# Index lists later, masks as bits and padded node rows in a four-layer graph attention kernel

## The chip, the cores and the metric

The kernel runs on one core of a Trainium2 chip. The metric is the device time of one execution in microseconds. A core has five engines, each with an instruction stream of its own that it takes in order: TensorE (PE, matmuls), VectorE (DVE), ScalarE (ACT), GpSimd (POOL, which here does almost nothing but issue indirect gathers) and SyncE (SP, which issues most other DMAs). [...]

## The reference

Four layers of graph attention over 4096 nodes with 256 features, each followed by a residual sum and a layer norm. `adj` is a 4096 x 4096 matrix in which about one entry in 256 is set, and the diagonal.

```python
# layers 0 and 1: 4 heads of 64; layer 2: 2 heads of 128, with its own scores
h    = (x @ W.T).reshape(C, H, D).transpose(1, 0, 2)
e    = leaky_relu(alpha_src[:, :, None] + alpha_dst[:, None, :], 0.2)
e    = where(adj[None, :, :] == 0, -inf, e)
out  = einsum('hij,hjd->hid', softmax(e, axis=-1), h)
# layer 3: one head of 256, attention of +e and of -e, then one matrix
new  = concatenate([softmax(e) @ x, -softmax(-e) @ x], axis=1) @ fc_W
out  = elu(new)
# after each layer
x    = layernorm(x + out)
```

## The kernel before

A **row tile** is 128 nodes (32 tiles in all), a **block** is four row tiles. For a row tile only the nodes matter that have an edge into it, and since edges are rare, the kernel packs them: for each partition it lists which row of each node tile to fetch. `lists()` makes these index lists (`idx`, 13 columns for each row tile) on the chip out of `adj`: the raw matrix is fetched (L387), turned into bytes on ACT (`bytes`, L393), folded into bits on DVE (`squeeze`, L405), and ranks, places and sums on PE and DVE give the list, written at L522. It is a generator: each `next(lists)` puts one step in the program; five steps fetch and fold one block and then every row tile has four.

A **projection** (`Projection`, six steps from `transpose` to `store`) turns the features of a row tile into its node values: a row of 260, 258 or 514 numbers of weighted values plus a few score terms, stored in DRAM as `vals` (L702), from where gathers take it. Scores for the other side go into `edge` (L714). In layer 0 a row begins with 16 words of list bits (`BITS`), stored by `squeeze` (L410).

`RowTile.load` (L754 to L765) brings in what a row tile needs: its scores `S`, its mask, its own node values, and by 13 indirect DMAs on POOL (L763) the rows that its lists name, six for half 0 and seven for half 1. Gathers of half 0 may read only rows below `MIX * 128` (tiles 0 to 22); those of half 1 may read all. `RowTile.half` then makes the weights on ACT (L880, L847 in layer 3), masks them on DVE (L837, L882, L849, L851) and multiplies on PE (L898). In layers 0 and 1 the mask bytes lie in PSUM; in layer 0 they are unpacked from gathered bits (`unpack`, L798), copied out (L822) and stored as `maskC`, which layers 1 to 3 read back.

Some blocks are not packed but done **whole** (`WHOLE`: block 7 in layer 1; 3, 7 and 6 in layer 2; 7 and 6 in layer 3): all 32 node tiles are read in order as `vw`, with mask bytes `mw` from `maskW`, 512 KB for eight node tiles (L1158, L1230). These units are spread over the steps of the row tiles (`Layer.whole`).

`Program.run` sets the order. In the **head**, 32 projections of layer 0 run as a pipeline with one step of each of six tiles in a turn, and list steps are woven in. Then follow layer 0's row tiles, with two list steps around each half, then layers 1 to 3. `Layer.part` loads the row tile at hand and the next one or two; buffers are pools (`g0`, `g1`: four gathers' slots each), and a scheduler moves instructions within each engine's stream.

Of the kernel before, what the change touches and what calls it, by code (L numbers as in the profile page):

```python
# [50 lines left out]
P = 128  # L51
# [31 lines left out]
LEAD = 4  # L83
MIX = 23
CAP = NPAIR * P
BW = BT * P // 32
# [15 lines left out]
ROW = tuple(b + v + 2 * t for b, v, t in zip(BITS, VALS, TERMS))  # L102
KEXP = 10.0
# [19 lines left out]
def kernel(ctx: ExitStack, tc: tile.TileContext, ins: dict, out: bass.AP):  # L123
# [15 lines left out]
        "maskC": dram.tile([NT, P, NU, P], U8, name="maskC"),  # L139
        "maskW": dram.tile([NB, P, NT, BT, P], U8, name="maskW"),  # L140
        "d": [const.tile([P, NT, TERMS[n]], F32, name=f"d{n}") if WHOLE[n] else None for n in range(4)],
        "v": [[dram.tile([N + 1, ROW[n]], F32, name=f"vals{n}{c}") for c in range(1 if n else 2)] for n in range(4)],
# [36 lines left out]
class Program:  # L179
# [99 lines left out]
    def lists(self, ctx):  # L279
# [33 lines left out]
        nc.vector.memset(ones, 1.0)  # L313
        upto, past = (cst.tile([P, P], F16, name=name) for name in ("upto", "past"))
# [9 lines left out]
        for c in range(3):  # L324
# [9 lines left out]
        steps = column("steps", ((0, 3 * NT, P),), [(c * NT, 0) for c in range(3)]  # L334
                       + [(3 * NT + c, -(NT - 1) * P) for c in range(2)])
# [6 lines left out]
        pat = cst.tile([P, 8, P // 32], I32, name="pat")  # L342
# [16 lines left out]
        shared["pat"] = pat  # L359

        limit = cst.tile([P, NP], F32, name="limit")
        nc.vector.memset(limit[:, :2 * FIRST], float(MIX * P - 1))
        nc.vector.memset(limit[:, 2 * FIRST:], float(N))
# [9 lines left out]
        class Block:  # L373
# [21 lines left out]
            def squeeze(self, part):  # L395
                js = slice(part * JG, (part + 1) * JG)
                if any(self.blk in w for w in WHOLE):
                    nc.sync.dma_start(out=shared["maskW"][self.blk, :, js], in_=self.mk)
# [9 lines left out]
                if part == BT - 1:  # L408
                    rows = shared["v"][0][self.blk % 2][:N, :BW].rearrange("(j p) w -> p j w", p=P)
                    nc.sync.dma_start(out=rows, in_=self.bits.rearrange("p j t w -> p j (t w)").bitcast(F32))  # L410

# [49 lines left out]
        class Places:  # L461
# [45 lines left out]
            def sum(self):  # L507
                for pos in range(NP):
# [7 lines left out]
                    nc.tensor.matmul(PX[:, pos:pos + 1], self.under[:, c * P:(c + 1) * P], ones[:, :1], start=True,  # L516
# [83 lines left out]
    def run(self):  # L600
        ins, nc = self.ins, self.nc
        nothing = self.small.tile([1, max(ROW)], F32, name="nothing")
        nc.vector.memset(nothing, 0.0)
        for n in range(4):
            for v in self.shared["v"][n]:
                nc.sync.dma_start(out=v[N:N + 1, :], in_=nothing[:, :ROW[n]])
        w0 = self.weights(0)
        layer = Layer(self, 0)
        with ExitStack() as ctx:
            lists = self.lists(ctx)  # L610
            xs = []
            for q in range(NT // 2):
                if q % 4 == 0:
                    slot = self.g0.tile([P, SLOT], F32, name="G")
                c = 2 * F * (q % 4)
                nc.sync.dma_start(out=slot[:, c:c + 2 * F].rearrange("p (t f) -> p t f", t=2),
                                  in_=to_tiles(ins["x"][2 * q * P:2 * (q + 1) * P, :]))
                xs += [slot[:, c:c + F], slot[:, c + F:c + 2 * F]]

            line = [Projection(self, 0, w0, x, m, (self.ptwo[0], self.ptwo[1], self.pmask)) for m, x in enumerate(xs)]  # L620
            turns, ahead, listed = NT + 5, BT + 1 + 4 * LEAD, 0
            for m in range(turns):
                while listed < ahead and listed * turns <= m * ahead:
                    next(lists)
                    listed += 1
                for k, step in enumerate(Projection.STEPS):
                    if 0 <= m - k < NT:
                        step(line[m - k])

# [8 lines left out]
        self.mwp = self.pool("mwp", 2)  # L638
# [5 lines left out]
        layer.close(None)  # L644


class Projection:
# [36 lines left out]
    def row(self):  # L684
        nc, n, sh = self.nc, self.n, self.shared
        H, D, T, A, m = HEADS[n], WIDTH[n] - 1, TERMS[n], LOGS[n], self.m
        row = self.prog.io.tile([P, ROW[n] - BITS[n]], F32, name="row", bufs=3)
        vals = row[:, :VALS[n]].rearrange("p (h c) -> p h c", h=H)
        self.terms = row[:, VALS[n]:].rearrange("p (k t) -> p k t", k=2)
# [19 lines left out]
    def store(self):  # L709
        n, nc, T = self.n, self.nc, TERMS[self.n]  # L710
        erow = self.prog.io.tile([4, P], F32, name="erow")
        shift = self.shared["shift3"] if n < 3 else self.shared["zero"]
        nc.scalar.activation(erow[:T, :], self.pe[:T, :P], AF.Identity, bias=shift[:T, LOGS[n]:LOGS[n] + 1])
        nc.sync.dma_start(out=self.shared["e"][n][self.m], in_=erow[:T, :])  # L714
# [8 lines left out]
class RowTile:  # L723
# [23 lines left out]
    def load(self, half):  # L747
# [4 lines left out]
        if half == 0:  # L752
            self.S = prog.ld.tile([P, H4, P], F32, name="S")
            nc.sync.dma_start(out=self.S[:, :TERMS[n]], in_=sh["e"][n][m].partition_broadcast(P))  # L754
            self.mk = prog.ld.tile([P, NU, P], U8, name="mk")
            if n > 0:
                nc.sync.dma_start(out=self.mk, in_=sh["maskC"][m])
# [1049 lines left out]
```

## Time and profile before

| | us |
|---|---|
| median of 3 runs | 2065.5 (2065.28 to 2066.7) |
| profiled execution | 2071.33 |
| its span, first to last instruction | 2069.6 |
| PE / DVE / ACT / POOL busy | 1822.6 / 1467.9 / 1500.9 / 1383.9 |
| DMA moved | 486.59 MB, 235 GB/s |

The profile tells of one execution. Its engine times are busy times; waiting and issuing are not in them, so an engine can be the limit at 67%. Gathers are the 1352 instructions of L763; with 13 to a tile they tell which row tile POOL is at. In a line of the timeline the columns are start, duration, engine, line, operation, output and inputs, and how many; in brackets stands how long the engine had been idle and what ended that. In a table of stretches each engine has its busy time and its number of instructions, then come the granted PE clock, the DMA share and GB/s.

### The profile page before, as it was taken

The page shows a single profiled execution, that of the slowest core. Times are in us where ns is not written, and L with a number is a line of the kernel's source. Part 1 is how long each engine was busy: PE and PEld are TensorE (multiplying, and loading weights), DVE is VectorE, ACT ScalarE, POOL GpSimd, SP SyncE. Part 2 cuts the span into 40 slices and gives each one's busy share as a digit, 9 for nine tenths or more (in the row PEclk, how much of TensorE's full clock was granted, in tenths as well). Part 3 has the DMA queues.
Part 4 walks back from the last instruction along what each step waited for, and adds up shares of the span by engine and source line. Part 5 has one row for each costly group of instructions (what it writes and reads, how often), then busy time and mean ns, then how long its engine had stood idle before and what let it go on. Part 6 is the DMA issues. An engine that isn't in the chain of part 4 may idle for free. (4 is left out here: it accounts for less than half of the span.)

```text
span 2069.6 us, 46290 instructions
## 1 busy us (share of the span) xinstructions
PE 1822.6 (88%) x15281; PEld 1509.8 (73%) x15281; DVE 1467.9 (71%) x4366; ACT 1500.9 (73%) x4659; POOL 1383.9 (67%) x1387
## 2 busy tenths in 40 slices
PE   4765798999899959989989998899998999999995
PEld 2444677777778859978878788788986677667773
DVE  2434888888888959977777867778876366575655
ACT  4436888888877948866767769878874687667873
POOL 0016777777777777777777767777762776666772
PEclk7666998989989979998999999999999899999998
DMA  8677999999986867766666766777875898888983
GB/s 287 177 187 253 316 300 328 269 294 318 328 207 179 236 197 201 207 191 188 192 187 187 203 176 187 231 209 229 233 205 188 262 297 274 261 289 276 294 254 109
DMA packets 297816, 486.59 MB, mean 235 GB/s; under 512 B 77815, under 2 KB 206940, under 8 KB 297565
## 3 DMA queue, kind: packets, MB, share of 16 engines
q1 hardware_dynamic: 218076, 251.50, 40.1%
q0 software_dynamic: 74880, 227.83, 38.0%
q10 hardware_dynamic: 4608, 4.20, 0.6%
q8 instruction: 123, 2.02, 0.4%
q14 instruction: 129, 1.05, 0.2%
HBM read 427.36 MB, written 55.99 MB: 234 GB/s over the span
## 5 line engine op out<-in xcount | busy, mean ns | idle before, releaser
L763 POOL DMA_INDIRECT G<-vals,idx x1352 | 1378.4, 1020 | 653.4 <-issue 348.9
L898 PE MATMUL bank<-G,w 128*64 128x130 f32 (+5 forms) x9156 | 943.5, 311 | 73.6 <-DVE w L837 64.2
L898 PEld LDWEIGHTS bank<-G,w 128*64 128x64 f32 (+1 forms) x9156 | 769.8, 162 | 226.3 <-DVE w L837 73.3
L880 ACT ACTIVATE w<-S,G 128x64 f32<-128x64 f32 (+1 forms) x3080 | 823.5, 351 | 133.2 <-DMA G<-vals,idx 84.2
L1181 PE MATMUL bank<-vw,pw 128*128 128x129 f32 (+1 forms) x2560 | 419.8, 322 | 17.5 <-DVE pw L1171 5.8
L1181 PEld LDWEIGHTS bank<-vw,pw 128*128 128x128 f32 x2560 | 374.1, 194 | 58.2 <-issue 16.0
L837 DVE SCALAR_TENSOR_TENSOR w<-w,bank 128x1024 f32<-128x1024 f32 (+1 forms) x240 | 322.5, 1344 | 13.0 <-ACT w L880 12.4
L673 PE MATMUL bank<-wext,xT 128*128 128x268 f32 (+3 forms) x640 | 188.3, 429 | 33.5 <-DVE row L699 24.1
L673 PEld LDWEIGHTS bank<-wext,xT 128*128 128x128 f32 x640 | 123.2, 210 | 61.2 <-DVE row L699 24.7
L847 ACT ACTIVATE w<-S,G 128x64 f32<-128x64 f32 (+1 forms) x329 | 105.3, 352 | 85.5 <-DMA G<-vals,idx 51.0
L1171 DVE SCALAR_TENSOR_TENSOR pw<-pw,mw 128x512 f32<-128x512 f32 x192 | 129.9, 687 | 36.9 <-ACT pw L1170 35.5
L1178 DVE TENSOR_TENSOR pw<-pw,mw 128x512 f32<-128x512 f32 x128 | 87.6, 688 | 96.1 <-ACT pw L1175 62.8
L393 ACT ACTIVATE mk<-raw 128x1024 uint8<-128x1024 int32 x128 | 130.3, 1051 | 32.6 <-DMA raw<-in_adjB_dram 32.3
L876 DVE TENSOR_TENSOR w<-S,G 128x384 f32<-128x384 f32 x180 | 92.4, 517 | 79.8 <-DMA G<-vals,idx 61.0
L1170 ACT ACTIVATE pw<-Sw,d 128x512 f32<-128x512 f32 x192 | 134.5, 710 | 15.5 <-PE bank L1181 10.2
L1244 PE MATMUL bank<-vw,pw 128*128 128x65 f32 x512 | 89.1, 257 | 19.9 <-issue 19.9
L1173 ACT ACTIVATE pw<-Sw,d 128x512 f32<-128x512 f32 x128 | 89.9, 708 | 19.3 <-DMA Sw<-edge 10.3
L1246 PE MATMUL bank<-pw,vw 128*65 128x128 f32 x512 | 99.5, 277 | 0.0
L1244 PEld LDWEIGHTS bank<-vw,pw 128*128 128x128 f32 x512 | 78.6, 194 | 27.6 <-issue 27.3
L1241 DVE SCALAR_TENSOR_TENSOR pw<-Sw,cw,mw 128x512 f32<-128x512 f32 x128 | 93.8, 740 | 0.0
L664 ACT COPY xT<-bank 128x256 f32<-128x256 f32 x128 | 46.3, 362 | 62.3 <-PE bank L659 41.0
L706 PE MATMUL bank<-ident,row 128*4 128x128 f32 (+2 forms) x128 | 37.6, 294 | 56.6 <-DVE row L693 30.5
(193 smaller groups left out, 1805.1 us busy)
## 6 DMA issues: line engine op xcount, KB each, us to landing
raw<-in_adjB_dram SPq DMA_DIRECT2D x128, 512.0 KB
G<-vals,idx POOLq DMA_INDIRECT x1352
mw<-maskW SPq DMA_DIRECT2D x36, 512.0 KB
vw<-vals SPq DMA_DIRECT2D x128, 128.5 KB
S<-edge SPq DMA_DIRECT2D x60, 256.0 KB
vals<-row SPq DMA_DIRECT2D x96, 134.0 KB
vw<-vals SPq DMA_DIRECT2D x96, 129.0 KB
xp<-y SPq DMA_DIRECT2D x96, 128.0 KB
```

The lines of the kernel that those rows point to most:

```text
L393: nc.scalar.activation(self.mk[:, 2 * q:2 * q + 2], src, AF.Copy)
L673: nc.tensor.matmul(pp[:, :c1 - c0], self.xT[:, k, :], wext[:, k, c0:c1], start=(k == 0), stop=(k == KT - 1 and brow is None))
L763: nc.gpsimd.indirect_dma_start(out=self.row(half, k), out_offset=None, in_=self.values[:N + 1 if half else MIX * P, :], in_offset=bass.Ind ...
L837: nc.vector.scalar_tensor_tensor(pair, pair, LEAST, mh2, op0=ALU.max, op1=ALU.mult)
L847: nc.scalar.activation(w[0][:, u, rows], S[:, 0, rows], AF.Relu, bias=d(g, 0))
L880: nc.scalar.activation(w[h][:, u, rows], S[:, h, rows], AF.Exp, bias=d(g, h))
L898: nc.tensor.matmul(a, w[h][:, u, rows], b, start=half == 0 and u == 0 and (n == 3 or h == turns[0][0]), stop=half == 1, skip_group_check=True)
L1170: nc.scalar.activation(p, S[:, h], AF.Exp, bias=d)
L1171: nc.vector.scalar_tensor_tensor(p, p, LEAST, mj, op0=ALU.max, op1=ALU.mult)
L1181: nc.tensor.matmul(accs[it][:, c:c + Wd], p[:, it, :], v[:, c:c + Wd], start=(j == 0 and h == heads[0]), stop=(j == NT - 1), skip_group_ch ...
L1244: nc.tensor.matmul(bu[:, it * Wd:(it + 1) * Wd], p[up][:, it, :], v[:, up * Wd:(up + 1) * Wd], start=j == 0 and it == 0, **how)
L1246: nc.tensor.matmul(bf[:Wd, it * P:(it + 1) * P], v[:, flat * Wd:(flat + 1) * Wd], p[flat][:, it, :], start=j == 0 and it == 0, **how)
```

## The change

1. *Head.* `LEAD` goes from 4 to 3: 17 list steps stand ahead of layer 0 for 21. Nine of them are woven into the first 24 turns of the projections (all 21 were spread over 37 turns), and eight follow after the projections. `x` comes in six DMAs for sixteen, layer 0's `edge` rows are stored four tiles at a time, the five small stores of zeros move from SP to ACT, and layer 0 prefetches one row tile ahead for two. `LATE` keeps a bound that `LEAD` had set.
2. *Masks.* `maskC` and `maskW`, bytes in DRAM, become `bitsC` and `bitsW`, 32 times 128 bits. Layer 0 copies out the gathered bits (28 words a half) and no longer the bytes; layers 1 to 3 unpack them on DVE for every half, and whole blocks for every node tile.
3. *Rows.* Node values stand `PITCH` apart: 320 words (1280 bytes) in layers 0 to 2, 520 words in layer 3, before 284, 268, 262 and 516. Indices are multiplied by 5 and count fifths of a row. Gathers move as many bytes as before; stores of `vals` write the pad, which is set to zero.

```diff
-LEAD = 4
+LEAD = 3
+LATE = 4
+MW = P // 32
+STRIDE = 5
+PITCH = tuple(-(-r // (u * STRIDE)) * u * STRIDE for r, u in zip(ROW, (64, 64, 64, 1)))
...
-            turns, ahead, listed = NT + 5, BT + 1 + 4 * LEAD, 0
+            turns, soon, listed = NT + 5, BT + 5, 0
             for m in range(turns):
-                while listed < ahead and listed * turns <= m * ahead:
+                while listed < soon and listed * 24 <= m * soon:
                     next(lists)
                     listed += 1
                 for k, step in enumerate(Projection.STEPS):
                     if 0 <= m - k < NT:
                         step(line[m - k])
+            for _ in range(BT + 1 + 4 * LEAD - listed):
+                next(lists)
...
-            for q in range(m, m + (3 if self.n == 0 else 2)):
+            for q in (m, m + 1):
...
+        nc.vector.memset(row[:, ROW[n] - BITS[n]:], 0.0)
...
-            self.mk = prog.ld.tile([P, NU, P], U8, name="mk")
+            self.bits = prog.ld.tile([P, 2 * HALF, MW], I32, name="bits")
             if n > 0:
-                nc.sync.dma_start(out=self.mk, in_=sh["maskC"][m])
+                nc.sync.dma_start(out=self.bits, in_=sh["bitsC"][m])
...
-                out=self.row(half, k), out_offset=None, in_=self.values[:N + 1 if half else MIX * P, :],
+                out=self.row(half, k), out_offset=None, in_=self.values[:N + 1 if half else MIX * P, :].rearrange("r (k c) -> (r k) c", k=STRIDE),
...
+        bits = self.bits[:, half * HALF:(half + 1) * HALF]
+        if L.n == 0:
+            t = self.m % BT * MW
+            rows = self.slot(half, 0)[:, :HALF * ROW[0]].bitcast(I32).rearrange("p (k c) -> p k c", k=HALF)
+            L.nc.vector.tensor_scalar(bits, rows[:, :, t:t + MW], 0, None, op0=ALU.bitwise_or)
+            if half == 1:
+                L.nc.sync.dma_start(out=L.shared["bitsC"][self.m], in_=self.bits)
...
-            if n == 0:
-                self.unpack(half, there.rearrange("p (t i) -> p t i", t=U))
-                nc.vector.tensor_scalar(kept, there, 0, None, op0=ALU.bitwise_or)
-                if half == 1:
-                    nc.sync.dma_start(out=sh["maskC"][self.m], in_=self.mk)
-            else:
-                nc.vector.tensor_scalar(there, kept, 0, None, op0=ALU.bitwise_or)
+            self.unpack(half, there.rearrange("p (t i) -> p t i", t=U))
+        else:
+            there = prog.mkp.tile([P, UNITS[1], P // 4], I32, name="mk")[:, :U]
+            self.unpack(half, there)
...
+    def block_bits(self, blk):
+        bits = self.prog.mwp.tile([P, NT, BT, MW], I32, name="bw")
+        self.nc.sync.dma_start(out=bits, in_=self.shared["bitsW"][blk])
+        return bits
+
+    def bytes(self, bits, j):
+        mj = self.prog.mup.tile([P, BT, P // 4], I32, name="mw")
+        spread(self.nc, mj, bits[:, j], self.shared["pat"])
+        return mj.rearrange("p t i -> p (t i)").bitcast(U8).rearrange("p (t i) -> p t i", t=BT)
```

`spread` is one DVE product: each word of bits, repeated over eight bit planes, is combined by `bitwise_and` with a pattern, which gives mask bytes. `unpack` calls it three times for a half, `bytes` once for a node tile.

## The prediction

> **What bounds the kernel now.** I read the table of stretches first, cut at the first GpSimd gathers of each layer (13 per row tile, so 416, 364, 260 and 312 for layers 0 to 3).
>
> ```profile
> core 0: us, PE busy (x) PEld busy (x) DVE busy (x) ACT busy (x) POOL busy (x), PEclk, DMA share, GB/s
> 125.00:165.00 40.00, 30.41 (x201) 19.71 (x201) 18.11 (x62) 12.17 (x39) 5.96 (x6) 0.59 0.66 144
> 165.00:698.00 533.00, 466.91 (x4671) 386.42 (x4670) 430.01 (x1279) 449.26 (x1524) 406.36 (x410) 0.88 0.94 281
> 698.00:1178.00 480.00, 428.11 (x4452) 383.28 (x4451) 381.91 (x982) 341.20 (x1300) 369.10 (x364) 0.94 0.70 196
> 1178.00:1545.00 367.00, 342.91 (x2988) 315.01 (x2989) 276.44 (x790) 290.76 (x865) 278.48 (x260) 0.97 0.75 214
> 1545.00:2070.00 525.00, 483.66 (x2640) 358.78 (x2636) 317.70 (x1091) 348.56 (x800) 319.53 (x313) 0.96 0.78 248
> ```
>
> No engine is full by this table, though POOL is: its timeline and the tile view of `vals` show why.
>
> ```profile
> L763 POOL DMA_INDIRECT G<-vals,idx x1352: 940/946/2292, 125.2 to 2036.3; - x194
>   issue: 348.9, 1112
> ...
> 131.74 0.95 POOL L763 DMA_INDIRECT G<-vals,idx  x1 [0.30 <-issue]
> 165.34 0.94 POOL L763 DMA_INDIRECT G<-vals,idx  x1 [32.65 <-DMA edge<-erow]
> 166.59 0.94 POOL L763 DMA_INDIRECT G<-vals,idx  x1 [0.30 <-issue]
> ...
> 1543.56 0.94 POOL L763 DMA_INDIRECT G<-vals,idx  x1 [0.30 <-issue]
> 1589.17 0.94 POOL L763 DMA_INDIRECT G<-vals,idx  x1 [44.67 <-ACT row L691]
> ```
>
> A gather takes 0.946 us and is followed by 0.304 us in which POOL waits for nothing: 1.25 us, 16.25 us for a tile's 13. From 165.3 to 1544.5 this runs on almost without another gap. So until layer 2 ends, the time is the start of this stream plus the number of gathers; whatever starts it earlier or lengthens a gather counts in full. The other waits in it are only the 9 us of one layer change. Layer 3 is different: PE is 92% busy, the chain of waits alternates between L898 and L1181, both PE, and POOL waits for PE to free slots.
>
> The stream starts at 165.3, not at 125.2, because half 1 of tile 0 may gather from all rows and so needs the last row stored:
>
> ```profile
> 147.49 1.53 SPq L702 DMA_DIRECT2D vals<-row  x2
> 161.31 0.79 SPq L702 DMA_DIRECT2D vals<-row  x2
> 162.76 0.80 SPq L702 DMA_DIRECT2D vals<-row  x2
> ```
>
> Layer 0 hides a second limit. The first three unpack products of a half (L798) mark where compute stands: 144 of them, 24 tiles, lie between 222.7 and 646.9, 17.67 us a tile, while POOL took 16.96 (24 tiles between 207.1 and 614.2). Compute falls behind, and what lets POOL run on is that its index lists are written early:
>
> ```profile
> 591.43 0.17 DVE L522 TENSOR_TENSOR idx<-bank,limit 128x13 int32<-128x13 f32 x1
> 597.72 0.94 POOL L763 DMA_INDIRECT G<-vals,idx  x1 [0.30 <-DVE total L454]
> ```
>
> That is tile 26: 6.3 us of lead. DMA isn't what slows compute there: the waits between 300 and 590 us are between PE, DVE and ACT, and the largest on a DMA is 4 us, though the DMA share is 1.0.
>
> **What the Trainium skill says.** "Perfetto Trace Analysis", section "DMA Instruction — SWDGE (GPSIMD)": the end of such a record is the end of descriptor generation, not of the transfer. The trace agrees: the median is 946 ns whether a row has 1048 or 2064 bytes. So the wider pitch should leave POOL's 1.25 us alone. "SBUF — State Buffer", section "SBUF: two separate sides": a VectorE operation with two SBUF inputs and a GpSimd operation exclude each other on a shared port. The trace agrees in size: gathers beyond 0.946 us sum to 369.1 - 364 x 0.946 = 24.8 us in layer 1 and 278.5 - 260 x 0.946 = 32.5 us in layer 2, where such products (L1241 and about half of L876, 137 us; L1171 and L882, 190 us) run: 0.17 to 0.18 us lost per us of product. "DMA: Bandwidth & Descriptors", section "How a descriptor splits into AXI transactions": a read that doesn't start on 256 bytes fetches an extra piece. Rows 1136, 1072 and 1048 bytes apart mostly start off it; 1280 always starts on it, 2080 doesn't. No view here isolates that.
>
> **The change part by part.** *Head.* In the built order, ACT makes its 24th mask conversion (L393, at 80.9 us before) with 9 of 32 rows begun; after, 14. The last 18 rows then have six single conversions between them, where the last 23 had 13 to 16 and the list work of tiles 1 to 5. Also gone before the last row: the second 64-byte store of list bits (issued 127.6; ACT then stood 8.45 us for a row store). Undisturbed rows took 1.6 us each (seven from 105.4 to 115.0). Sum: 80.9, less 2 (five small stores leave SP's queue, x comes in 6 DMAs for 16), plus 5 rows x 1 us of transfers, plus 18 x 1.6 = 29, plus 6 x 2 for a conversion and its wait, plus 3 for landing: 128. The stream starts 37 us earlier.
>
> *Layer 0.* The lists are postponed, not removed. Built order: an index list stood 2.0 to 2.5 unpacked tiles ahead of use; after, 1.0 to 1.67. Taking one tile, 17.7 us, off the lead shown (22 to 28 us around tile 8, 6 at tile 26), POOL must wait from about tile 10, and the layer goes at compute's pace. So the gain is compute's. Its first exponentials (L880) were at 177.0; after, six conversions and the bits store stand before them, so about 16 us past the new start: 144, gain 33. Tiles 0 to 3 now carry lists (before, six lists were ready): -6. Each tile then saves 0.2 us of DVE: the copies L822 go (0.283 + 0.312), two copies of 28 words come (priced as the 0.156 us of L693) and a pad memset (0.06): +5 over 24 tiles. Lists end one tile later and the last list holds POOL: -5. Layer 1 starts 27 us earlier. If the lead holds after all, 37; if the head gains less, 10.
>
> *Masks as bits, layers 1 to 3.* Per row tile six products: 2 x 0.213 + 3 x 0.192 + 0.260 = 1.26 us (L798 by form); per whole-block step one of 128 words, 0.28 (L416). Layer 1: 28 x 1.26 + 64 x 0.28 = 53 us of DVE, of which the removed L826 gives back 17. Layer 2: 20 x 1.26 + 96 x 0.28 = 52. Layer 3: 24 x 1.26 + 128 x 0.28 = 66. DVE has room (80, 75 and 61% busy), so the time itself lies beside gathers and matmuls; the cost is gathers lengthened. Short products may slip between a gather's accesses (0) or cost as the long ones do (0.18, or 0.35 as an upper end, twice that). I take 0.15: 8 us in layer 1, 8 in layer 2. The layer change at 1545 to 1589, where PE is full and DVE at 85%, takes 3; layer 3, PE-bound, 2. Together 21 us, 12% of the 171 added.
>
> *Transfers.* Counted from the issue list: mask bytes written and read were 6.3 + 18.9 + 4.7 + 10.6 = 40 MB; the bits take about 5.4; pads add 2.4. Some 33 of 487 MB go. Nothing that ends POOL's stream waits for them: cost and gain zero, bounds 0 and -10 (shorter landings in layer 3, where ACT waited 51 us for gathers). Grouped edge stores, pad memsets in layers 1 to 3 and the prefetch of two tiles for three: zero, behind POOL.
>
> *Sum.* -27 + 21 = -6 on the execution's own 2071.3 us (span 2069.6). The median of the runs is 2065.5, so 2059.5; I say 2059.
>
> **The rivals.** *A, slower: DVE's added work gets on the path.* Its place is layers 1 to 3. Layer 0 shows that compute falls behind POOL with DVE 81%, ACT 84% and PE 88% busy; layer 2 would have DVE at 89% and PE at 93%. If a quarter of the 171 us lands on the path, 43 - 27 = +16: 2081. It decides from 16% (27/171). Against it: after its opening stall layer 2 did some tiles in under 14 us. *B: layer 0 swallows the head.* If compute starts late and lists cost more, the gain is 10: 10 - 21 = +11, 2076. For it: layer 0's pace; against: fewer conversions really precede the last row. *C: transfers matter more.* Aligned reads and 33 MB less shorten landings, POOL's lead holds: -37 - 10 + 13 = -34, 2031. Against: no DMA wait in the views is on POOL's stream. That the pitch cuts rows into several descriptors, lengthening each gather, I give almost nothing: only the index's coefficient changes in the instruction.
>
> **How the numbers follow.** Forecast 0.47 (2045 to 2072 by the terms' own bounds), A 0.25, B 0.12, C 0.16. The range 2036 to 2084 leaves out a tenth on each side. No change can be told within 0.2%, 4 us. Forecast: 0.29 faster, 0.10 same, 0.08 slower; A 0.02, 0.02, 0.21; B 0.02, 0.02, 0.08; C 0.15, 0.01, 0. Sum 0.48, 0.15, 0.37.
>
> **What would show it.** The seventh gather near 128 us; waits of POOL on DVE from tile 10 of layer 0; layer 1's first gather near 671; mean gathers of 1.04 us in layer 1 and 1.10 in layer 2; layer 3's length unchanged within 5 us. Wrong would be: a seventh gather after 145, no POOL waits in layer 0, or a layer 2 whose compute trails POOL by more than a tile.

## The result, and the profile after

The changed kernel takes 2166.1 us (2159.5 to 2168.8, four executions) where the kernel before took 2065.4 (2064.1 to 2066.7): a ratio of 1.048, 95% interval 1.046 to 1.051. The forecast was 2059. On two of the chips used below the kernel before itself took 2733 and 2779 us, so the experiments from there are compared only with others on the same chip.

The chain of row starts reads best from the first gather of each layer. All numbers are us from the start of the profiled execution; layer 3's length runs to the end of the span.

| | 7th gather | layer 1 starts | layer 1 | layer 2 | layer 3 | span |
|---|---|---|---|---|---|---|
| before | 165.3 | 698.2 | 480.0 | 411.0 | 480.4 | 2069.6 |
| after | 126.4 | 767.1 | 480.4 | 407.7 | 508.0 | 2163.1 |

The head gives 39 us. Layer 0 then takes 640.7 us from its seventh gather to layer 1's first, where it took 532.8: 108 us lost. Layers 1 and 2 are as long as they were, within 4 us, and layer 3 is 28 us longer. The two losses are in two places. For both the runs point to the order of instructions within the engines; for the first this is shown by a single edit, for the second it is inferred.

This is the table of stretches of the changed kernel, cut at the seventh gather, at the first gathers of layers 1 and 2, and where layer 2's gathers end.

```profile
core 0: us, PE busy (x) PEld busy (x) DVE busy (x) ACT busy (x) POOL busy (x), PEclk, DMA share, GB/s
126.00:767.00 641.00, 496.73 (x4876) 405.72 (x4877) 441.40 (x1365) 458.87 (x1552) 399.30 (x410) 0.83 0.75 226
767.00:1247.00 480.00, 430.09 (x4456) 378.88 (x4456) 405.25 (x1198) 338.31 (x1295) 369.29 (x364) 0.95 0.65 183
1247.00:1613.00 366.00, 340.41 (x2958) 311.63 (x2954) 300.72 (x1021) 290.02 (x855) 286.64 (x261) 0.97 0.67 190
1613.00:2163.00 550.00, 494.48 (x2616) 355.94 (x2616) 363.57 (x1363) 347.32 (x797) 330.69 (x313) 0.95 0.73 218
```

In layer 0 no engine is near full: PE is busy 497 us of 641 and VectorE 441. The layer is longer because all of them wait. The list of waits between 200 and 760 us (engine and line, what it waited for, us in all, times, longest) says on what:

```profile
engine line waited for: us in total, times, longest us
PEld bank L911 <- DVE w L850: 125.2, 54, 11.5
...
DVE bits L809 <- DMA G<-vals,idx: 102.3, 22, 10.3
...
POOL G L785 <- DVE idx L528: 72.5, 5, 14.8
```

TensorE waits for VectorE's mask product, VectorE waits at the copy of the bits (L809) for gathers, and GpSimd waits for VectorE to write an index list (L528). That is a ring. The page's group line of the copy shows how cheap it looks if only its own time is read (busy us, mean ns, then idle time of the engine before it):

```profile
L809 DVE TENSOR_SCALAR bits<-G 128x28 int32<-128x28 int32 x64 | 11.3, 178 | 129.4 <-DMA G<-vals,idx 122.5
```

64 copies cost 11.3 us of work and 122.5 us of standing. One turn of the ring, in the timelines of GpSimd and VectorE around the gathers of tile 13 and tile 14 (start, duration, and in brackets the idle time before with its releaser):

```profile
388.24 0.95 POOL L785 DMA_INDIRECT G<-vals,idx  x1 [0.31 <-issue]
403.96 0.94 POOL L785 DMA_INDIRECT G<-vals,idx  x1 [14.77 <-DVE idx L528]
...
385.89 0.29 DVE L409 SCALAR_TENSOR_TENSOR bits<-fold 128x128 int32<-128x128 int32 x1
394.11 0.18 DVE L809 TENSOR_SCALAR bits<-G 128x28 int32<-128x28 int32 x1 [7.92 <-DMA G<-vals,idx]
...
403.51 0.17 DVE L528 TENSOR_TENSOR idx<-bank,limit 128x13 int32<-128x13 f32 x1 [2.28 <-ACT counts L443]
```

Tile 13's last gather ends on GpSimd at 389.2. VectorE waits for its data until 394.1 and only then makes the copy. The work queued behind the copy takes until 403.5, when the list of tile 14 is written; tile 14's first gather follows at 404.0. No gather of tile 14 could overlap those of tile 13. Over four tiles (first gathers of tile 12 and tile 16: 348.99 and 437.08) this makes 88.1 us where 4 x 16.25 = 65 would do, so 23 us are lost in these four tiles.

The **built order**, the fixed sequence in which each engine takes its instructions, shows that this is no accident of timing; the trace has the same sequence. In VectorE's stream the list of tile 14 is the 20th instruction behind the copy of tile 13's second half, and the lists of tiles 10, 18, 22 and 26 stand just so. List 10 stands behind the copies of tiles 0 to 9, and lists 13 and 14, 17 and 18, and so on up to 26 stand behind all copies of the tile before.

In the kernel before, the products that unpack the gathered bits (L798) write the one bank of masks, and the copy L822 read that bank, so neither came early. Sums that need only gathered rows and scores (L876) stood in VectorE's stream too, but between 200 and 690 us VectorE waited for gathers 4.3 us in all, where it now waits 102.3 at the copy alone. When a list is written there, the mask products done are 2.5 to 3.0 tiles behind it.

### The profile page after: what moved, and what is told of

It reads as the page before. It is cut to its first block, busy times and chain, and to the rows that moved or that the text cites. A ratio compares the mean times of both kernels' runs of the same rounds, so it can differ in the third digit from the quotient of the medians.

```text
span 2163.1 us, 46803 instructions
## 1 busy us (share of the span) xinstructions
PE 1843.4 (85%) x15281; PEld 1505.3 (70%) x15281; DVE 1559.7 (72%) x5159; ACT 1497.8 (69%) x4659; POOL 1396.3 (65%) x1387
## 4 chain that ended last, share of the span: by engine, by line
PE 46%; POOL 12%; DVE 11%; DMA 11%; ACT 10%; issue 8%; SPq 1%; DVEq 0%; POOLq 0%; ACTq 0%
PE bank L911 24%; POOL G L785 12%; PE bank L1192 11%; DMA G<-vals,idx 8%; ACT w L893 6%; PE bank L690 4%; DVE w L850 3%; ACT mk L399 1%; ACT pw L1181 1%; PE bank L1255 1%; DMA raw<-in_adjB_dram 1%; PE bank L1253 1%; PE bank L522 1%; PE bank L524 1%; DVE pw L1182 1%
## 5 line engine op out<-in xcount | busy, mean ns | idle before, releaser
L911 PE MATMUL bank<-G,w 128*64 128x130 f32 (+5 forms) x9156 | 964.7, 314 | 177.6 <-DVE w L850 141.9
L1192 PE MATMUL bank<-vw,pw 128*128 128x129 f32 (+1 forms) x2560 | 413.7, 320 | 11.5 <-DVE pw L1182 4.0
L809 DVE TENSOR_SCALAR bits<-G 128x28 int32<-128x28 int32 x64 | 11.3, 178 | 129.4 <-DMA G<-vals,idx 122.5
L1250 DVE SCALAR_TENSOR_TENSOR pw<-Sw,cw,mw 128x512 f32<-128x512 f32 x128 | 93.1, 743 | 0.0
```

Source lines behind the costliest of these rows:

```text
L911: nc.tensor.matmul(a, w[h][:, u, rows], b, start=half == 0 and u == 0 and (n == 3 or h == turns[0][0]), stop=half == 1, skip_group_check=True)
L1192: nc.tensor.matmul(accs[it][:, c:c + Wd], p[:, it, :], v[:, c:c + Wd], start=(j == 0 and h == heads[0]), stop=(j == NT - 1), skip_group_ch ...
```

## The experiments

Each experiment is an edit of the changed kernel unless it says otherwise. The stage lengths of all are in one table at the end of this section.

### The list lead, or the copy

The first pair changes the lead of the lists, with the prefetch of three tiles that goes with it, and then the place of the copy in the program's text, with the products reading the gathered rows directly.

```diff
-LEAD = 3
+LEAD = 4
...
-            for q in (m, m + 1):
+            for q in range(m, m + (3 if self.n == 0 else 2)):
```

> The changed kernel with the list lead put back: 4 x 4 list steps ahead instead of 4 x 3 before layer 0 starts, and layer 0's prefetch of three tiles instead of two; the head's early weave and everything else stay. Theory 1 (a postponed list is late at POOL): POOL's five waits on the index write, 72 us, go; layer 1's first gather comes near 690 instead of 767, and the total near 2089. Theory 2 (the copy of the gathered bits, which stands in VectorE's order ahead of the next list and waits for a transfer, makes the loop): the lead moves only the first waits, layer 1 starts near 750 and the total stays above 2145. Layer 3 keeps its 508 us under both.

Measured: 2191.4 us, ratio to before 1.061 (1.057 to 1.064), layer 1 at 800.8. A longer lead is no cure; GpSimd waits 90.7 us for lists in nine places instead of 72.5 in five. In the built order lists are now 2.5 to 3 tiles ahead of the mask products, as before the change, but lists 13, 14, 17, 18 and so on still stand behind the copies of the tile just before. The layer became 34 us longer than with lead 3. In the trace lists 12, 16, 20 and 24 now stand behind a copy of the tile just before too, and GpSimd stands idle for 8 us before each of these tiles, which it did not with lead 3.

```diff
-            L.nc.vector.tensor_scalar(bits, rows[:, :, t:t + MW], 0, None, op0=ALU.bitwise_or)
-            if half == 1:
-                L.nc.sync.dma_start(out=L.shared["bitsC"][self.m], in_=self.bits)
+            kept, bits = bits, rows[:, :, t:t + MW]
...
         spread(L.nc, words[:, u:u + len(FULL[half]), :], bits[:, k:k + len(FULL[half])], pat)
+        if L.n == 0:
+            L.nc.vector.tensor_scalar(kept, bits, 0, None, op0=ALU.bitwise_or)
+            if half == 1:
+                L.nc.sync.dma_start(out=L.shared["bitsC"][self.m], in_=self.bits)
```

> The changed kernel, list lead 3 as it is, but layer 0's products read the masks in the gathered rows directly, as before the change, and the copy of the bits for layers 1 to 3 follows the products instead of preceding them. Theory 2: VectorE's wait of 109 us at the copy goes, layer 1 starts near 700, total near 2100. Theory 1: the products wait for the same transfer at the same place; layer 1 starts within 10 us of 767 and the total within 0.5% of 2166. Layer 3 keeps its 508 us under both.

Measured: 2165.3 us, 1.047 (1.043 to 1.051), layer 1 at 775.7. Taken at its word this would speak against the copy. But the built order shows that the edit moved nothing: the scheduler places instructions by what they need, the copy needs only the gather, and it stands ahead of the same lists as in the changed kernel (10, 13, 14, 17 and so on). The experiment did not test what it was made for. To move the copy, its place has to be held by an **edge**: a dependency that lets one instruction be issued only after another.

### Which part of the change brings the loss

The next two take one part back: the head (lists, loads of x, edge stores, lead and prefetch as before), and the pitch.

```diff
-            for tiles in (2, 2, 4, 8, 8, 8):
+            for q in range(NT // 2):
...
-            turns, soon, listed = NT + 5, BT + 5, 0
+            turns, soon, listed = NT + 5, BT + 1 + 4 * LEAD, 0
...
-        k = self.m % 4 if n == 0 else 0
+        k = 0
```

> The kernel before with masks as bits and the wide pitch, without the head (list steps, lead, prefetch, loading of x and edge stores as before). If the loss of layer 0 comes from the head's lead alone: first seven gathers at 165, layer 1 near 698, layer 2 near 1178, layer 3's 508 us stay, total near 2093. If the copy of the bits makes it: layer 1 at 730 or later, total above 2120. If layer 3's 27.6 us come from the head, layer 3 takes 481 and the total is near 2066.

Measured: 2200.0 us, 1.064 (1.060 to 1.068), layer 1 at 812.9, layer 3 at 501.7. Without any of the head, and with its lead of 4, layer 0 loses more than with it. So the head isn't the cause in either place.

```diff
-STRIDE = 5
-PITCH = tuple(-(-r // (u * STRIDE)) * u * STRIDE for r, u in zip(ROW, (64, 64, 64, 1)))
+STRIDE = 1
+PITCH = ROW
```

> The changed kernel with node values at the old distance (1136, 1072, 1048 and 2064 bytes), head and bits kept. The forecast's reading, that the pitch moves nothing on the path: within 0.3% of 2166, layer 3 at 508. If the pitch shortens landings that layer 0's loop waits for (3.87 to 3.18 us was seen): layer 1 starts later by up to 32 x 0.7 = 22 us, 2188. If the pitch of 2080 bytes makes layer 3 longer: layer 3 at 481, 2139.

Measured: 2235.7 us, 1.082 (1.078 to 1.086). Layer 1 starts at 862.0, 95 us later, a result that no expectation covered; layer 3 takes 476.5 us. Layer 3's loss comes with the pitch, then, and in layer 0 the bits cost even more without it. The trace shows where: the lists stand behind the same copies, but ten more of VectorE's instructions stand between copy and list (30 for 20 at tiles 10, 14, 18, 22 and 26, and 13 for 3 at tiles 13, 17, 21 and 25), so that the four tiles from 12 on take 98.4 us for 88.1. GpSimd's idle times before tiles 4 to 6 (23.5, 11.8 and 17.3 us for 4.0, 1.4 and 5.1) are most of the rest.

### Holding the copy in its place

The same edit as in the second experiment, with one edge: the copy may not be issued before the last product of its half.

```diff
-        spread(L.nc, words[:, u:u + len(FULL[half]), :], bits[:, k:k + len(FULL[half])], pat)
+        last = spread(L.nc, words[:, u:u + len(FULL[half]), :], bits[:, k:k + len(FULL[half])], pat)
+        if L.n == 0:
+            with L.prog.tc.issue_after(last.ins):
+                L.nc.vector.tensor_scalar(kept, bits, 0, None, op0=ALU.bitwise_or)
```

It was made at lead 3, at lead 4 with the prefetch of three tiles, and at lead 4 without the pitch.

> The changed kernel with one edge of order more: layer 0's products read the masks in the gathered rows, and the copy of the bits is held behind the last of these products of its half on VectorE. The list lead stays at 3. In the built order the copies then stand 1.0 to 2.0 tiles behind the list they used to stand in front of by 0 to 1.0. Theory of order (a copy that waits for tile k-1's gathers stands ahead of the write of list k, so that gathers of two tiles in four can't overlap): the waits of POOL on the index write fall below 25 us in all and layer 1's first gather comes near 700 instead of 767, total near 2100. Rival, the list lead of 3: VectorE would wait at the first product instead, layer 1 after 745, total above 2144. Layer 3 stays at 500 to 510 us under both.

> The same edge, with the list lead of 4 and layer 0's prefetch of three tiles put back; the head's early weave stays. Theory of order: layer 0 keeps its old pace and the 39 us of the head arrive, layer 1's first gather near 665 (698 less 39, plus lists that come later), total near 2065. Rival, that the bits cost VectorE time on the path: layer 1 not before 700. Against the run with lead 4 and the copies in front (800 us, 2191) the edge alone would be worth 130 us.

> The run with the copies held behind and lead 4, with the old distances of 1136, 1072, 1048 and 2064 bytes. If the pitch works in the memory (layer 0 at 862 without it against 767 with it): layer 1's first gather 30 us or more later than in the run with the pitch. If that too was a matter of order: layer 1's first gather within 10 us of that run. Layer 3 at 476 to 482 us, so the total near 2035 in the second case.

On the chip on which the kernel before took 2733 us, these three measured 2774.6, 2770.4 and 2728.3, ratios of 1.015 (1.009 to 1.022), 1.015 (1.011 to 1.020) and 0.998 (0.996 to 1.001). Layer 1 started near 1000 us in all, so they decided nothing on layer 0. They were run again.

> The same kernel as in the run with the copies held behind and lead 4, again, because in that call the kernel before itself took 2733 us instead of 2066, with long waits that no semaphore shows. Theory of order: layer 1's first gather near 665, layer 3 at 500 to 510 us, total near 2065. Rival, that the bits cost VectorE time on layer 0's path: layer 1 not before 700.

Measured: 2041.9 us, 0.986 (0.983 to 0.989), layer 1 at 647.5, 50.7 us earlier than in the kernel before and 153 earlier than with lead 4 and the copies in front. The view of the copy's line in this run:

```profile
L820 DVE TENSOR_SCALAR bits<-G x64: 165/175/181, 152.2 to 655.3; 128x28 int32<-128x28 int32 x64
its engine sat idle before it (us, times) until:
who waited for it (us, times):
```

The copies still take 0.175 us each, and the list of waits before them is empty. The table of stretches has the rest: layer 0 from the seventh gather on now takes 523 us, with the busy times of the changed kernel within 7% on every engine.

```profile
core 0: us, PE busy (x) PEld busy (x) DVE busy (x) ACT busy (x) POOL busy (x), PEclk, DMA share, GB/s
124.00:647.00 523.00, 464.77 (x4868) 380.45 (x4868) 444.11 (x1369) 458.52 (x1550) 398.38 (x410) 0.91 0.89 277
```

> The kernel with the copies held behind at a list lead of 3, again, because in its first call every kernel was slowed. If lead 3 with copies behind suffices: layer 1 within 10 us of the 647.5 of lead 4, total near 2045. If the lead costs something of its own, as the forecast had it (POOL waits for lists from tile 10 on, layer at compute's pace, 12 us of the head lost): layer 1 at 660 to 675, total near 2060. If the lead were the main cause: layer 1 after 700.

Measured: 2047.2 us, 0.993 (0.991 to 0.995), layer 1 at 654.7. This run and the second experiment differ by the edge alone: it is worth 118 us of the total and 121 of layer 1's start (on their two chips the kernel before took 2062 and 2069 us). The lead of 3 costs 6 us of layer 0 against the lead of 4, not the main part. With lead 3 a list is written as little as 0.3 us before its first gather (tiles 6, 18 and 22), with lead 4 at least 7.1 from tile 6 on; GpSimd stands 1.2 us at most for it, at tile 6 with lead 3.

> The same kernel as before without the pitch, copies held behind, lead 4, again for the same reason. If the pitch works in the memory: layer 1's first gather 30 us or more later than in the run with the pitch. If the 95 us that the pitch was worth in layer 0 were the loop's: within 10 us of it. Layer 3 at 476 to 482 us; total near 2035 in the second case.

Measured: 2034.5 us, 0.984 (0.981 to 0.987), layer 1 at 659.2, layer 3 at 478.2. So most of the pitch's 95 us was the ring's; 12 us remain, 7 of them before the seventh gather (131.3 against 124.0).

> The kernel without the head (first lists, loads of x, edge stores and lead as before the change), masks as bits with the copies held behind, wide pitch in fifths of a row. If the head's gain is the 39 us of the seventh gather: layer 1 near 647 + 39 = 686, and the total near 2081 with layer 3's 508. If the head is worth less than its seventh gather shows: layer 1 nearer to 650. If bits and pitch bring nothing to layer 0: 698.

Measured: 2069.4 us, 1.003 (1.002 to 1.005), layer 1 at 676.2, its seventh gather at 152.0. Against the run with the head (124.0, 647.5) the head is worth 28 us at both places: all that reaches the seventh gather reaches layer 1. That is 28 of the 41 us by which the seventh gather now comes earlier than in the kernel before; the other 13 came from bits and pitch, whose effect on the head had been put at nothing.

### Layer 3: one engine's order, two engines', all

Layer 3's length goes with the pitch in every run so far. The built order differs there too. On TensorE, V stands for a matmul of the whole blocks and G for one of row tiles (the trace records each of them twice):

```
before, and without the pitch:  V30 G14 V10 G14 V12 G14 V24 G14 V12 ... G14 V4 G14 V4 G14 V4 G42
changed:                        V41 G14 V14 G14 V61 G14 V3 G14 V2 ... G14 V11 G14 V9 G126
```

On ScalarE the copy of z of a finished tile stands right behind the exponentials of a half in the first case, and after three to five sums of the next half in the second. The waits of the changed kernel in layer 3 show an engine waiting in its order for others:

```profile
engine line waited for: us in total, times, longest us
ACT z L1338 <- DVE recp L1335: 78.1, 21, 8.9
...
POOL G L785 <- PE bank L911: 66.1, 38, 8.0
PEld bank L911 <- issue: 60.5, 107, 5.5
```

First an edge was to bring this copy of z back to its old place on ScalarE and VectorE, with TensorE left as it was.

```diff
+            with ExitStack() as order:
+                if self.n == 3:
+                    for ins in (self.tile(m).exps, self.tile(m).masked):
+                        order.enter_context(self.prog.tc.issue_after(ins.ins))
-            self.tile(m - 1).finish()
+                self.tile(m - 1).finish()
```

> The changed kernel with edges in layer 3 alone: the finish of the tile before is held behind the first half's exponentials on ScalarE and behind its mask products on VectorE. In the built order of before and of the run without the pitch ScalarE's z copy stands right behind these exponentials, in the changed kernel among the next half's sums, three to five of them in front. Theory of order: ScalarE's wait for the reciprocal (78 us) falls below 25 and layer 3 takes 478 to 488 us instead of 508, total near 2142. Rival, that rows 2080 bytes apart are slower to move: layer 3 stays within 5 us of 508. Layer 1's first gather stays near 767.

> The kernel with layer 3's finish held behind the exponentials on ScalarE and the mask products on VectorE, again, because in its first call every kernel was slowed. TensorE keeps the changed kernel's order, with 126 row-tile matmuls at the end. Since TensorE's order alone did not help and all engines' order together did, mending two engines and leaving TensorE should not help either: layer 3 at 500 or more, total 2160 or more. If ScalarE's wait for the reciprocal were the cause: layer 3 near 482, total near 2142.

Both runs fell on the two chips named above: 2794.4 us, 1.023 (1.018 to 1.027), and 2825.3, 1.017 (1.013 to 1.022). Layer 3 took 564.0 us in the first, on the chip where a run with its old order took 517.6 and runs with the changed kernel's order 543.5 and 547.9, so this edge did not shorten it. In the trace neither engine has its old order back. In the second the wait for the reciprocal fell, and the slots that TensorE frees late stayed:

```profile
POOL G L785 <- PE bank L911: 80.9, 33, 9.5
...
ACT z L1342 <- DVE recp L1339: 26.3, 7, 6.9
```

Then an edge for TensorE alone, in the changed kernel and with the copies held:

```diff
-        self.whole(2 * m + part)
+        with ExitStack() as order:
+            if self.n == 3 and hasattr(self.tile(m), "product"):
+                order.enter_context(self.prog.tc.issue_after(self.tile(m).product.ins))
+            self.whole(2 * m + part)
```

> The changed kernel with one edge in layer 3 alone: the whole blocks' matmuls of a half step are held behind the row tile's matmuls of that half on TensorE. In the built order of before, and of the run without the pitch, 14 row-tile matmuls alternate with 8 or 12 of the whole blocks down to the last three halves; in the changed kernel 61 of the whole blocks stand in a row near the start and 126 row-tile matmuls at the end with none between. The edge brings the even order back, ScalarE's z copies stay among the sums. Theory, TensorE's order makes layer 3 long: layer 3 at 478 to 488 us, total near 2142. Rival, ScalarE's order: 500 or more. Rival, transfers of rows 2080 bytes apart: 500 or more, and waits for gathers come instead of waits for TensorE.

> Both edges: copies behind the products and lead 4 in layer 0, TensorE's even order in layer 3, head, bits and pitch kept. If both theories of order hold, their gains add: layer 1 near 665, layers 1 and 2 as long as in the changed kernel (480 and 408), layer 3 near 482, total near 2038, some 1.3% below the kernel before. If either is wrong, 2065 or more.

Measured: 2189.4 us, 1.059 (1.056 to 1.062), and 2068.1, 1.001 (0.999 to 1.002), with layer 3 at 527.4 and 530.2. TensorE's old order alone is not enough, then: it was back but for one pair of halves, and the layer was 20 us longer still. Nor was it tested by itself, as the edge changed the orders of VectorE and ScalarE too. The waits moved:

```profile
POOL G L785 <- PE bank L911: 84.2, 43, 6.4
...
ACT z L1341 <- DVE recp L1338: 60.3, 18, 7.1
...
PEld bank L911 <- DVE w L862: 54.5, 15, 22.0
```

TensorE now waits up to 22 us for masks that VectorE and ScalarE make in another order. That left two causes: all engines' orders together, or the 2080 bytes. They come apart with the unit of the index. The change counts it in fifths of a row, so the gather names pieces of 256 and, in layer 3, 416 bytes. Quarters give the same distances of 1280 and 2080 bytes with pieces of 320 and 520.

```diff
-STRIDE = 5
-PITCH = tuple(-(-r // (u * STRIDE)) * u * STRIDE for r, u in zip(ROW, (64, 64, 64, 1)))
+STRIDE = 4
+PITCH = tuple(-(-r // (u * STRIDE)) * u * STRIDE for r, u in zip(ROW, (16, 16, 16, 2)))
```

With this, the built order of layer 3 is that of the run without the pitch: in the traces TensorE's matmuls, ScalarE's instructions and VectorE's 1162 from the layer's first gather on are the same one by one. The page counts the same packets and bytes for the gathers' queue either way:

```profile
q0 software_dynamic: 74880, 227.83, 36.9%
```

```profile
q0 software_dynamic: 74880, 227.83, 39.0%
```

The first is the changed kernel's, the second that of the next run, which has the copies held and lead 4 as well; only the share of the shorter span differs.

> The run with the copies held behind and lead 4, but the unit in which the index counts is a quarter of a row instead of a fifth. Rows stay 1280 bytes apart in layers 0 to 2 and 2080 in layer 3; only the view that the gather names changes (units of 320 and 520 bytes for 256 and 416), and with it the built order: in layer 3 all engines stand as in the kernel before. Theory of order: layer 3 at 476 to 483 us instead of 508, total near 2014. Rival, that 2080 bytes are slower to move than 2064: layer 3 stays at 500 to 510, total near 2042. Layer 1's first gather within 8 us of 647.5.

Measured: 2013.6 us, 0.977 (0.975 to 0.978), layer 3 at 477.7, layer 1 at 650.4. This is the fastest of all. The waits of its layer 3:

```profile
engine line waited for: us in total, times, longest us
...
ACT w L863 <- DMA G<-vals,idx: 50.0, 58, 5.6
...
PEld bank L914 <- issue: 32.9, 99, 0.6
...
POOL G L785 <- PE bank L914: 24.5, 22, 3.8
...
ACT z L1341 <- DVE recp L1338: 17.0, 12, 4.2
```

ScalarE waits for gathers again, as in the kernel before, and no longer for the reciprocal. TensorE's busy time in stretches of 60 us, counted from the layer's first gather, shows what that is worth; the second half of the changed kernel's layer 3, then the middle of this one's:

```profile
core 0: us, PE busy (x), PEclk, DMA share, GB/s
...
1835.00:1895.00 60.00, 52.87 (x277) 0.94 0.77 228
1895.00:1955.00 60.00, 59.50 (x311) 1.00 0.83 253
1955.00:2015.00 60.00, 51.61 (x272) 0.94 0.77 229
2015.00:2075.00 60.00, 59.47 (x317) 1.00 0.81 232
2075.00:2135.00 60.00, 48.65 (x255) 0.89 0.75 212
```

```profile
core 0: us, PE busy (x), PEclk, DMA share, GB/s
...
1712.00:1772.00 60.00, 53.14 (x273) 0.91 0.80 241
1772.00:1832.00 60.00, 60.00 (x329) 1.00 0.89 275
1832.00:1892.00 60.00, 60.00 (x324) 1.00 0.88 262
1892.00:1952.00 60.00, 60.00 (x330) 1.00 0.85 257
```

The changed kernel starts its last whole-block matmul 431 us into the layer (at 2085.7) with 126 row-tile matmuls still to come, the other at 443 with 42. From 2085.7 on TensorE has row tiles only, and in the end stretch (2075 to 2135) it is idle for 11 of 60 us.

> The changed kernel with nothing but the index unit of a quarter of a row, distances 1280 and 2080 bytes kept. Theory: layer 3 at 476 to 483, total near 2138, layer 1 still near 767 since the copies and lists stand there as in the changed kernel. Rival, as above: 2160 or more.

Measured: 2132.8 us, 1.035 (1.033 to 1.037), layer 3 at 476.8, layer 1 at 771.1. On the changed kernel itself the unit takes 31 us off layer 3, more than its 28 us of loss, and leaves the other stages within 6 us.

No run has the unit of 416 bytes with the old order, so that the order, and not the unit itself, makes the layer long is inferred. Two things in the traces speak for it. From the end of a gather's record to the end of its last packet, layer 3's gathers take 2.9 us on average in the changed kernel, with the unit of 416 bytes, and 3.1 with that of 520, so the smaller unit is not slower to land. And the long waits of the changed kernel's layer 3 are for TensorE's slots and for the reciprocal, not for gathers.

> The fastest run so far with rows 2304 bytes apart in layer 3 instead of 2080, a whole multiple of 256 bytes; order as in that run but for one matmul. If the start of a row matters to layer 3's transfers: landings shorter than the 3.1 us of that run, and, as layer 3 waits 50 us for gathers on ScalarE, up to 10 us less in all: near 2004. If it doesn't: within 0.3% of 2014.

Measured where the kernel before took 2779 us: 2785.5 us, 1.002 (1.000 to 1.004), layer 3 at 520.7 us. In the trace a few instructions of VectorE and ScalarE have other places too. With no other run of this order on that chip, it says nothing on the distance in layer 3, and that stays open.

### All stages

Every row is one profiled execution of the run named, with the median of all its executions in the last column; the runs on the two chips named above are left out.

| | 7th gather | layer 1 starts | layer 1 | layer 2 | layer 3 | median |
|---|---|---|---|---|---|---|
| before | 165.3 | 698.2 | 480.0 | 411.0 | 480.4 | 2065.4 |
| after | 126.4 | 767.1 | 480.4 | 407.7 | 508.0 | 2166.1 |
| lead 4 | 126.5 | 800.8 | 479.5 | 405.7 | 503.4 | 2191.4 |
| copy moved in the text | 126.9 | 775.7 | 479.3 | 412.3 | 503.5 | 2165.3 |
| no head | 154.5 | 812.9 | 484.3 | 409.5 | 501.7 | 2200.0 |
| no pitch | 133.0 | 862.0 | 480.2 | 413.3 | 476.5 | 2235.7 |
| copy held, lead 4 | 124.0 | 647.5 | 483.3 | 405.2 | 507.8 | 2041.9 |
| copy held, lead 3 | 125.3 | 654.7 | 477.2 | 403.1 | 510.7 | 2047.2 |
| copy held, lead 4, no pitch | 131.3 | 659.2 | 478.6 | 416.4 | 478.2 | 2034.5 |
| copy held, no head | 152.0 | 676.2 | 480.8 | 403.9 | 503.5 | 2069.4 |
| TensorE's order held | 124.8 | 772.2 | 476.7 | 404.9 | 527.4 | 2189.4 |
| both held | 125.3 | 650.4 | 477.2 | 407.9 | 530.2 | 2068.1 |
| quarters of a row | 124.5 | 771.1 | 477.3 | 406.0 | 476.8 | 2132.8 |
| copy held, lead 4, quarters | 126.3 | 650.4 | 478.0 | 403.7 | 477.7 | 2013.6 |

Wherever the copy is held, layer 0 takes 524 to 529 us from the seventh gather to layer 1; before the change it was 533. Its 410 gathers at 1.25 us make 513 of that: it is bound by the gathers again, and the head counts in full.

## Why the prediction was wrong

It said 6 us faster and the kernel is 101 slower. By its steps:

*The head.* The number was right, the seventh gather put at 128 and coming at 126.4, but in part by luck. The sum gave all 37 us to the conversions and rows of the head; the runs give the head 28 us and bits and pitch 13.

*Layer 0.* This is the step that failed. It put layer 1 27 us earlier, and it came 69 later: 96 us of the miss. (Layers 1 and 2 came out 22 us shorter than forecast, layer 3 25 us longer.) The failing sentence is "two copies of 28 words come (priced as the 0.156 us of L693)". The price was right, 0.178 us. What was not looked at is what such a copy waits for and what stands behind it. It needs only a gather that has landed, so the scheduler could place it ahead of the next index list, in VectorE's fixed order; then the list waits for the gathers before it, and GpSimd waits for the list. The edge that holds the copy behind the products, and nothing else, turns 2165.3 us into 2047.2. The prediction did foresee GpSimd's waits on VectorE from tile 10, and they came exactly there (14.2 us at tile 10). It gave them to the shorter lead and to compute's pace. That mechanism is worth some 6 us: layer 0 with lead 3 against lead 4, the copies held. A prediction can name the right symptom with the wrong cause; what would have told them apart beforehand is the order of copies and lists, which needs no execution.

*Masks as bits in layers 1 to 3.* Forecast +8, +8, +3 and +2. Layer 1 came out at +0.4, layer 2 with the layer change at -3.3. The mean gather was put at 1.04 us in layer 1 and at 1.10 in layer 2; it was 369.29/364 = 1.015 and, by the gathers' own records, 1.102. The added products lengthened nothing in layer 1. The Trainium skill, "SBUF — State Buffer", section "SBUF: two separate sides", has a VectorE product of two SBUF inputs and a GpSimd operation that reads SBUF exclude each other. The prediction's 0.15 us per us came from the long products. In layer 1 the unpack products (L659, 0.18 to 0.33 us each) took 52.8 us of VectorE and GpSimd's busy time rose by 0.2 us, so here the measurement decides that short products cost next to nothing. The trace agrees: gathers longer than 1 us have a long product of a whole block (L1250, 0.74 us) beside them for 42% of their time and other gathers for 12%, but L659 for 15 and 11%. In layer 2 the records grew by 8 us in this execution, and without the pitch the stage took 413.3 and 416.4 us for 411.0: 2 to 5 us where 11 were forecast, which the pitch then covers.

*Transfers and pitch.* Put at nothing, with a gain of 10 us as the bound. Here the second failure lies: "cost and gain zero" for the pitch, and "layer 3, PE-bound, 2". Layer 3 grew by 28 us with the pitch. The bytes and distances are not the cause, as quarters of a row keep them and take 476.8 to 477.7 us. The unit of 416 bytes in the gather's view went with another order of TensorE, VectorE and ScalarE in layer 3, in which the whole blocks' matmuls bunch early and leave the last row tiles alone. What in the scheduler turns a unit of 416 bytes into that order wasn't examined. The pitch's own gain is small: with the copies held, layer 0's seventh gather comes 7 us and layer 1 12 us earlier with it than without it, and layer 2 takes 403.1 to 412.3 us in the eleven runs with it against 411.0 to 416.4 in the three without. Inside the ring it went with an order in which fewer instructions stand between copy and list, and there it saved 95 us; why the scheduler built that order was not examined either.

*The rivals.* None held. The slower one, that 16% of VectorE's added work lands on the path in layers 1 to 3, left no trace: with quarters of a row these layers take 1360 us together, where they took 1371 before. The second, that layer 0 swallows the head, had the right place, but it foresaw 11 us in all where 101 came. The faster one needed GpSimd's lead to hold, and it did not. A rival "an added instruction is placed ahead of the producer of the bottleneck's input" was missing.

## What to carry to other kernels

An added instruction can cost what it makes those behind it wait for, and not only what it takes: before pricing a short copy of freshly loaded data at its duration, find in the built order which instruction behind it on the same engine feeds the unit that bounds the stage. Where a scheduler makes the order, compare the orders of all engines in every stage, even for an edit of an address or a unit that moves no byte; moving a line in the text may move nothing, and an edge on one engine can make things worse where the orders of several belong together. Then put the copy behind its neighbours by an edge: here that, and a unit of a quarter of a row, turned 4.8% slower into 2.3% faster, with the lists' lead and layer 0's prefetch as before and the rest of the change kept.

## What the runs showed of the hardware

Gathered rows that start on 256 bytes land a little sooner in layer 0 and hardly in layers 1 and 2. From the end of a gather's record to the end of its last packet took 3.39 us on average in layer 0 with the pitch and 3.73 without it (copies held, lead 4, same chip), 2.18 against 2.21 in layer 1, and 2.23 in both in layer 2.
